# A quarter of the state-times-C products of the last two scan blocks on GpSimd, read from a state that the scan writes to SBUF

## The chip, the cores and the metric

One core of one Trainium2 chip. The metric is the device time of the core in microseconds; the lower the better. Engines are named as in the profile: PE (matrix products), DVE (VectorE), ACT (ScalarE), POOL (GpSimd), SP (the engine that issues most DMAs here).

## The reference

Four layers in a row work on x of 4 sequences x 1024 tokens x 256 channels in float32, each adding its normalised output to x: a linear-attention encoder of four layers, a LoRA mixture, a Mamba layer (a selective state space), and a mixture of 8 experts. The change is in the Mamba layer:

```python
def step(h, inp):
    u, d, b, c = inp
    dA = jnp.exp(d[..., None] * A)
    h = h * dA + (d * u)[..., None] * b[:, None, :]
    y = jnp.einsum('bds,bs->bd', h, c)
    return (h, y)
h0 = jnp.zeros((Bb, D_IN, D_STATE), dtype=x.dtype)
_, ys = jax.lax.scan(step, h0, (u_t, d_t, B_t, C_t))
```

There are D_IN = 512 channels with D_STATE = 16 states each, so the state h has 8192 numbers, and a recurrence along the 1024 tokens of every sequence. After the scan, y goes through a projection and a layer norm; then comes the gating of the experts, and tokens are sent to their expert's slots in memory (disp), worked on, and added into the output by a scatter.

## The kernel before, in words

The kernel builds a list of operations, and a planner (`Program.order`) decides the order on every engine. It goes through the list by a clock of its own: every operation has a cost from a table (`VECTOR_NS`, `GPSIMD_NS`, `SCALAR_NS`), an engine takes the operation that can start first, and buffers of a pool are handed out by their planned times. `emit` then writes all engines' instructions in that order. So each engine runs a fixed queue in order, and one changed cost or one operation on another engine can change the order of everything recorded with it. Where the planner sees PE idle for long it adds idle matrix products (`fill`, seen in the profile as mm<-cst).

Tokens are cut into 8 blocks of 512 (NBLK = 8, TB = 512), two to a sequence (NB = 2; half = 0 for the first). The encoder runs over units of one layer and one block; beside it `stream` feeds the later layers, block after block: `front(j)` makes the inputs of the scan, `scan(j)` does the recurrence, `back(j)` the projection and norms, `route(j)` the gating, and `expert(k)` one expert. The encoder is through before the last blocks; with the scans of blocks 6 and 7 the experts run (from j == NBLK - 2 on). The front of block 7 runs beside the scan of block 6.

`scan(j)` goes over the block's 8192 states in 64 tiles of 128 partitions x 512 tokens; a tile holds 16 channels with 8 states each. The loops are db (4 groups of 128 channels), r (2), q (4) and k (2 halves of the states); k = 0 and 1 make a pair. Each tile takes these steps:

- SP loads dd: delta, and delta times u, spread over partitions (three buffers each, once a pair).
- POOL makes dbu = (delta u) x B (tag dbu, three buffers in SBUF).
- ACT makes h = exp(A delta) in PSUM (`ps_h`, two buffers).
- DVE scans along the tokens: h = h x state + dbu, in place in PSUM (`tensor_tensor_scan`).
- In the first half of a sequence (blocks 0, 2, 4, 6) DVE copies the last column of the state to last_h, from which the second half starts.
- DVE makes hc = h x C (eight buffers in SBUF).
- PE sums hc over the states into y (`sums`, four tiles q side by side).

After the last r, DVE makes ys from y, and POOL multiplies ys by the gate zl. In the profile, bc is the tile of B or C.

Nearly every instruction is recorded by one helper line (L207), so groups are told apart by their tiles. Before the change the steps in question are lines 1259 (dbu), 1266 (scan), 1271 and 1272 (hc).

Of the kernel before, what the change touches and what calls it, by code (L numbers as in the profile page):

```python
# [12 lines left out]
ALU = mybir.AluOpType  # L13
# [8 lines left out]
TB = 512  # L22
NT = TB // P
NBLK = BATCH * SEQ // TB
LAYERS = 4
NB = SEQ // TB
# [408 lines left out]
def sandwich_kernel(ctx: ExitStack, tc: tile.TileContext, io: dict):  # L435
    nc = tc.nc
# [38 lines left out]
    nc = Program(tc)  # L475
# [121 lines left out]
    def layers(ctx: ExitStack):  # L597
# [615 lines left out]
        def scan(j):  # L1213

            half = j % NB
            BC = []
            for side in range(2):
                t = fpool.tile([P, NSH, TB], F32, tag=f"bc{side}", name=f"bc{side}")
                nc.sync.dma_start(
                    t, bcd[j][side].unsqueeze(0).to_broadcast([GC, SH, NSH, TB])  # L1220
                )
                BC.append(t)
            Bt, Ct = BC
            begun.append(j)
            ys = Y[j] = fpool.tile([P, NDB, TB], F32, tag="ys", name="ys")
            for db in range(NDB):
                y = ps_y.tile([P, TB], F32, tag="y", name="y")

                def sums(tiles, r, k):
                    start = r == 0 and k == 0  # L1230
                    stop = r == GQ - 1 and k == NSH - 1
                    nc.side_by_side(
                        [
                            (y[q * 32 : (q + 1) * 32, :], m["gsum"][:, r, :], tiles[q, k], start, stop)
                            for q in range(4)
                        ]
                    )

                late = []
                for r in range(GQ):  # L1240
                    if r == GQ // 2:
                        xl = fpool.tile([P, TB], F32, tag="xl", name="xl")
                        nc.sync.dma_start(xl, xcd[j][db])
                        zl = fpool.tile([P, TB], F32, tag="zl", name="zl")
                        nc.sync.dma_start(zl, zsd[j][db])
                    tiles = {}
                    for q in range(4):
                        g = q * GQ + r
                        gg = db * (P // GC) + g
                        dd = []  # L1250
                        for k in range(2):
                            t = spool.tile([P, TB], F32, tag=f"dd{k}", name=f"dd{k}", bufs=3)
                            nc.sync.dma_start(
                                t,
                                dud[j][db][g * GC : (g + 1) * GC, k, :].unsqueeze(1).to_broadcast([GC, SH, TB]),
                            )
                            dd.append(t)
                        for k in range(NSH):
                            dbu = spool.tile([P, TB], F32, tag="dbu", name="dbu", bufs=3)
                            nc.gpsimd.tensor_tensor(dbu, dd[1], Bt[:, k, :], ALU.mult)  # L1260
                            h = ps_h.tile([P, TB], F32, tag="h", name="h")
                            nc.scalar.activation(
                                h, dd[0], AF.Exp, scale=m["A"][:, gg, k : k + 1]
                            )
                            last = m["last_h"][:, gg, k : k + 1]
                            nc.vector.tensor_tensor_scan(
                                h, h, dbu, 0.0 if half == 0 else last, ALU.mult, ALU.add
                            )
                            if half < NB - 1:
                                nc.vector.tensor_copy(last, h[:, TB - 1 : TB])  # L1270
                            hc = tiles[q, k] = spool.tile([P, TB], F32, tag="hc", name="hc", bufs=8)
                            nc.vector.tensor_tensor(hc, h, Ct[:, k, :], ALU.mult)
                            if late:
                                sums(*late.pop(0))
                        yield 4
                    late = [(tiles, r, k) for k in range(NSH)]
                for args in late:
                    sums(*args)
                t = ys[:, db, :]
                nc.vector.scalar_tensor_tensor(  # L1280
                    t, xl, m["mcol"][:, db, M_D : M_D + 1], y, ALU.mult, ALU.add
                )
                nc.gpsimd.tensor_tensor(t, t, zl, ALU.mult)
                yield 0.8
# [340 lines left out]
        def stream():  # L1625
# [10 lines left out]
            for j in range(NBLK):  # L1636
# [16 lines left out]
                for n, cost in enumerate(scan(j)):  # L1653
                    yield cost
                    post()
                    if extra:
                        if (got := next(extra[0], "end")) == "end":
                            extra.pop(0)
                        else:
                            yield got  # L1660
                    if n % 2 == 0 or j == NBLK - 1:
                        if side:
                            got = next(side[0], "end")
                            if got == "end":
                                side.pop(0)
                            else:
                                yield got
                        elif ready == j and nxt is None and j + 1 in closed:
                            nxt = front(j + 1)
                            side.append(nxt)  # L1670
                            ready = j + 1
# [199 lines left out]
```

## Time and profile before

| what | us |
|---|---|
| median of 3 runs | 2727.3 |
| lowest and highest run | 2727.06, 2740.75 |
| the profiled execution | 2735.95 |
| its span | 2734.1 |
| scan of block 6 on DVE, first start to last end | 2374.3 to 2534.4 |
| scan of block 7 on DVE | 2540.5 to 2705.7 |
| busy in the span: PE, DVE, ACT, POOL | 2524.7, 1726.9, 1590.6, 1325.1 |

The page of the profile gives each engine's busy time and its costliest groups. Over the whole span PE is busy 92% of the time, because the encoder runs for most of it. The last two scan blocks are a stage of their own, from 2374 us to 2706 us, followed by 28 us in which the last block is projected, normalised and stored. What the change is worth is read from this stage alone: the table by stretches gives the busy time of each engine there, the groups say what ended the idle time ahead of each kind of instruction, and the timeline shows the loop.

### The profile page before, as it was taken

How to read it: one execution, taken by the hardware profiler on the slowest of the kernel's cores; microseconds unless marked ns; L12 is line 12 of the kernel's file. 1: busy time of each engine (PE TensorE's matmuls, PEld its weight loads, DVE VectorE, ACT ScalarE, POOL GpSimd, SP SyncE). 2: the span in 40 equal slices, each digit the busy share in tenths (PEclk: the TensorE clock that was granted, in tenths of full speed). 3: DMA queues.
4: the chain of work that ended last, by engine and by line, in shares of the span. 5: the costliest groups of instructions: out<-in, count | busy, mean ns of one | idle time of the engine just before them, and what ended most of it. 6: DMA issues, size and time to landing. Idle time of an engine off the chain costs nothing. (4 is left out here: it accounts for less than half of the span.)

```text
span 2734.1 us, 31975 instructions
## 1 busy us (share of the span) xinstructions
PE 2524.7 (92%) x9794; PEld 1568.9 (57%) x9794; DVE 1726.9 (63%) x3291; ACT 1590.6 (58%) x3309; POOL 1325.1 (48%) x1845
## 2 busy tenths in 40 slices
PE   9999999999999999999999998988998998888996
PEld 6566556656656555556655555555554566444664
DVE  2121322223468766885349887997897994599885
ACT  4434454456676666665666776765765643666443
POOL 1101111123255455564427467764864883467865
PEclk9999999999999999999999999998998999899998
DMA  4011201121354343442245445545444453767762
GB/s 108 27 46 56 66 27 32 51 66 66 105 168 148 104 153 121 147 147 85 85 136 167 134 148 174 177 150 176 135 151 155 129 151 101 246 193 234 207 179 53
DMA packets 202227, 342.18 MB, mean 125 GB/s; under 512 B 32197, under 2 KB 79514, under 8 KB 198976
## 3 DMA queue, kind: packets, MB, share of 16 engines
q1 hardware_dynamic: 197760, 334.80, 39.2%
q0 software_dynamic: 4288, 5.27, 1.1%
q8 instruction: 79, 1.29, 0.2%
q14 instruction: 100, 0.82, 0.1%
HBM read 281.13 MB, written 59.92 MB: 125 GB/s over the span
## 5 line engine op out<-in xcount | busy, mean ns | idle before, releaser
L207 POOL TENSOR_TENSOR dbu<-dd,bc 128x512 f32<-128x512 f32 x512 | 664.2, 1328 | 267.6 <-DVE h L207 224.0
L207 ACT ACTIVATE h<-dd,A 128x512 f32<-128x512 f32 x512 | 344.5, 687 | 295.8 <-DVE hc L207 293.9
L207 PE MATMUL mm<-w,fT 128*128 128x256 f32 x2176 | 490.7, 383 | 5.7 <-ACT t L207 2.7
L207 PEld LDWEIGHTS mm<-w,fT 128*128 128x128 f32 x2176 | 413.8, 192 | 85.8 <-issue 15.5
L207 DVE TENSOR_TENSOR_SCAN h<-h,last_h,dbu 128x512 f32<-128x512 f32 x256 | 321.3, 1279 | 53.1 <-ACT h L207 39.7
L207 DVE TENSOR_TENSOR hc<-h,bc 128x512 f32<-128x512 f32 x512 | 340.8, 679 | 16.3 <-PE y L242 14.7
L207 DVE TENSOR_TENSOR_SCAN h<-h,dbu 128x512 f32<-128x512 f32 x256 | 304.3, 1218 | 33.0 <-ACT h L207 27.1
L398 PE MATMUL mm<-cst 128*128 128x256 f32 x1166 | 274.7, 394 | 7.5 <-DVE qe L207 3.3
L207 PE MATMUL mm<-hT,w1b 128*128 128x512 f32 (+1 forms) x576 | 255.7, 589 | 18.0 <-ACT fT L207 9.1
L207 PE MATMUL mm<-hT,w1a 128*128 128x512 f32 (+1 forms) x576 | 258.3, 596 | 14.5 <-ACT hT L207 12.1
L398 PEld LDWEIGHTS mm<-cst 128*128 128x128 f32 x1166 | 228.3, 198 | 58.3 <-issue 17.2
L207 PE MATMUL mm<-wkv,hT 128*128 128x512 f32 x512 | 228.1, 597 | 8.3 <-DVE qT L207 6.1
L207 ACT ACTIVATE fT<-mm,cols 128x512 f32<-128x512 f32 x256 | 170.8, 681 | 72.1 <-PE mm L207 71.6
L207 DVE TENSOR_TENSOR X<-X,mm 128x512 f32<-128x512 f32 x128 | 87.1, 681 | 185.7 <-PE mm L207 185.4
L207 PEld LDWEIGHTS mm<-hT,w1b 128*128 128x128 f32 x576 | 107.7, 193 | 163.0 <-issue 100.2
L207 POOL TENSOR_TENSOR X<-X,ro 128x1024 f32<-128x1024 f32 x64 | 151.4, 2372 | 80.5 <-ACT tok L207 57.4
L207 POOL TENSOR_SCALAR ve<-mv 128x4 f32<-128x4 f32 (+1 forms) x105 | 20.4, 195 | 345.9 <-DVE mv L207 333.4
L207 PEld LDWEIGHTS mm<-hT,w1a 128*128 128x128 f32 x576 | 108.0, 196 | 137.7 <-issue 93.4
L207 ACT ACTIVATE tok<-X,nb,rs 128x256 f32<-128x256 f32 x288 | 149.6, 591 | 32.7 <-POOL nb L207 31.7
L207 PEld LDWEIGHTS mm<-wkv,hT 128*128 128x128 f32 x512 | 97.2, 191 | 123.4 <-issue 105.4
L207 ACT ACTIVATE tok<-tok,nb,rs 128x256 f32<-128x256 f32 x252 | 131.9, 590 | 48.2 <-POOL nb L207 43.6
L207 ACT ACTIVATE r<-mv,eps 128x4 f32<-128x4 f32 (+1 forms) x105 | 30.9, 295 | 220.5 <-DVE mv L207 220.3
(195 smaller groups left out, 4037.0 us busy)
## 6 DMA issues: line engine op xcount, KB each, us to landing
dd<-dud SPq DMA_DIRECT2D x512, 256.0 KB
w<-in_w_dram SPq DMA_DIRECT2D x16, 1024.0 KB
dud<-t SPq DMA_DIRECT2D x32, 512.0 KB
tok<-in_x_dram SPq DMA_DIRECT2D x16, 512.0 KB
wkv<-in_wkv_dram SPq DMA_DIRECT2D x16, 512.0 KB
w1a<-in_w_dram SPq DMA_DIRECT2D x16, 512.0 KB
w1b<-in_w_dram SPq DMA_DIRECT2D x16, 512.0 KB
t<-in_w_in_dram SPq DMA_DIRECT2D x16, 512.0 KB
```

The lines of the kernel that those rows point to most:

```text
L207: getattr(getattr(self.nc, engine), name)(*map(put, args), **{k: put(v) for k, v in kwargs.items()})
L398: self.nc.tensor.matmul(tile[:, 0:IDLE_COLS], work[:, 0:P], work, start=True, stop=True)
```

## The change

For j >= 6 and q == 3 the scan writes its state to the dbu tile in SBUF, in place of dbu, instead of to h in PSUM. For these tiles the product hc is made on GpSimd, which reads the state and C from SBUF. The copy to last_h reads the state from where it now lies: in block 6 that makes 16 copies out of SBUF. All other tiles stay as they were. Of 64 tiles of a block 16 are concerned, in two blocks 32.

```diff
@@ -1263,13 +1263,17 @@
                                 h, dd[0], AF.Exp, scale=m["A"][:, gg, k : k + 1]
                             )
                             last = m["last_h"][:, gg, k : k + 1]
+
+                            share = j >= NBLK - NB and q == 3
+                            state = dbu if share else h
                             nc.vector.tensor_tensor_scan(
-                                h, h, dbu, 0.0 if half == 0 else last, ALU.mult, ALU.add
+                                state, h, dbu, 0.0 if half == 0 else last, ALU.mult, ALU.add
                             )
                             if half < NB - 1:
-                                nc.vector.tensor_copy(last, h[:, TB - 1 : TB])
+                                nc.vector.tensor_copy(last, state[:, TB - 1 : TB])
                             hc = tiles[q, k] = spool.tile([P, TB], F32, tag="hc", name="hc", bufs=8)
-                            nc.vector.tensor_tensor(hc, h, Ct[:, k, :], ALU.mult)
+                            engine = nc.gpsimd if share else nc.vector
+                            engine.tensor_tensor(hc, state, Ct[:, k, :], ALU.mult)
                             if late:
                                 sums(*late.pop(0))
```

## The prediction

> **What bounds the kernel now.** I read the table of stages first, cut where a state-scan block begins and ends on VectorE (DVE), because the change touches only the last two blocks. Its columns are the stretch, its length, then busy time of PE, PEld, DVE, ACT and POOL, the clock, the DMA share and GB/s:
>
> ```profile
> 2374.20:2534.40 160.20, 141.13 (x546) 75.69 (x544) 153.82 (x249) 105.97 (x227) 114.66 (x107) 0.96 0.77 227
> 2534.40:2540.50 6.10, 6.10 (x34) 4.04 (x31) 1.54 (x5) 1.73 (x5) 2.70 (x4) 1.00 1.05 283
> 2540.50:2705.70 165.20, 154.53 (x690) 104.25 (x688) 139.06 (x208) 77.78 (x177) 118.54 (x127) 0.96 0.55 157
> 2705.70:2734.10 28.40, 8.55 (x42) 5.15 (x36) 11.29 (x27) 6.04 (x16) 10.98 (x31) 0.74 0.13 29
> ```
>
> Block 6 is DVE-bound: 153.82 of 160.20 us, 96%. Block 7 has DVE at 84%, so waits matter there. The last 28 us are a chain of small steps that the change does not touch. PE looks fuller than either, but the groups of PE show 55.1 us of idle fillers (mm<-cst), so it is not the limit. GpSimd (POOL) is at 72% in both blocks.
>
> Next, the groups of DVE in block 7 say what ends its idle time:
>
> ```profile
> L207 DVE TENSOR_TENSOR_SCAN h<-h,last_h,dbu 128x512 f32<-128x512 f32 x64 | 80.3, 1280 | 12.5 <-POOL dbu L207 6.9 <-ACT h L207 5.0 <-issue 0.4
> L207 DVE TENSOR_TENSOR hc<-h,bc 128x512 f32<-128x512 f32 x63 | 41.1, 678 | 5.9 <-PE y L242 5.6
> L207 DVE SCALAR_TENSOR_TENSOR pp<-ex,pp 128x3 f32<-128x3 f32 x4 | 0.7, 176 | 9.5 <-ACT X L207 9.5
> ```
>
> Already 6.9 us go to waiting for GpSimd's dbu, and 15 us to two stalls behind expert work (PE y, ACT X). The groups of GpSimd for blocks 6 and 7:
>
> ```profile
> L207 POOL TENSOR_TENSOR dbu<-dd,bc 128x512 f32<-128x512 f32 x62 | 84.3, 1427 | 25.5 <-DVE h L207 23.1 <-DMA dd<-dud 2.3
> L207 POOL TENSOR_TENSOR dbu<-dd,bc 128x512 f32<-128x512 f32 x63 | 84.9, 1457 | 17.0 <-DVE h L207 4.9 <-DVE short L207 2.9 <-DVE sm_s L207 1.9
> ```
>
> So GpSimd has about 23 us of real slack in block 6 (waiting for the scan to free a dbu buffer) and about 17 us in block 7. Last, the timeline of DVE, where the loop runs undisturbed in block 7, and the rows of tile run, which hold a copy between SBUF tiles:
>
> ```profile
> 2677.70 2.45 DVE L207 TENSOR_TENSOR_SCAN h<-h,last_h,dbu 128x512 f32<-128x512 f32 x2
> 2680.07 1.26 DVE L207 TENSOR_TENSOR hc<-h,bc 128x512 f32<-128x512 f32 x2
> 2681.57 2.47 DVE L207 TENSOR_TENSOR_SCAN h<-h,last_h,dbu 128x512 f32<-128x512 f32 x2 [0.23 <-issue]
> ```
> ```profile
> L207 DVE COPY run<-run x7: 160/164/1872, 1151.8 to 2612.0; 128x8 f32<-128x8 f32 x7
> ```
>
> A pair of tiles costs 3.87 us: two scans (2.38 from start to start of what follows), two products (1.19, so 0.595 each) and 0.23-0.3 waiting for ACT to refill the two PSUM tiles h.
>
> **The change part by part.**
>
> *Removed from DVE.* Per block 4 x 2 x 2 = 16 products hc, 32 in all, at 0.595 us in sequence: 9.5 us a block, 19.0 us together. In block 6 DVE is the limit, so this is on the path.
>
> *Added to GpSimd.* The same 32 products from SBUF. The nearest row is dbu, the same shape and operands: 1.27 us alone, 1.24 us in a row. 16 x 1.25 = 20 us a block: 114.66 becomes 134.7 in block 6, 118.54 becomes 138.5 in block 7. The cover is the 23 and 17 us of slack; 20 us just fits the one and not the other.
>
> *The scan writes dbu in SBUF instead of h.* No row has a scan that writes SBUF. The product reads PSUM and writes SBUF at 678 ns, while mm<-sg,mm writes PSUM at 686 ns: the destination costs nothing there. I take 0 and bound it at +-0.05 us a scan, +-1.6 us in all.
>
> *The h tile comes free after the scan instead of after the product.* ACT's exp for the next pair then no longer waits for hc; the 0.23 us after a shared pair goes, 8 times, in block 7 only (in block 6 other DVE work fills it): -1.8 us. What is late next is dbu: the third row below.
>
> *dbu is held longer.* There are three buffers, and the product on GpSimd now frees two of them. Walk a shared pair in block 7 from its first scan at 0. The scans end at 1.28 and 2.47. GpSimd does hc 1.35-2.6, hc 2.6-3.85, and only then dbu for the second tile of the next pair, 3.85-5.1 (the changed program's GpSimd order has just this: hc, hc, dbu). DVE scans the first tile of the next pair 2.38-3.6, does its product to 4.25, then waits to 5.15, scans, multiplies: 6.95 us at the next pair. Before, the two pairs took 2 x 3.87 = 7.74. The gain is 0.8 us, not 1.19 + 0.23 = 1.42, times 8: 6.4 us in block 7 instead of 9.5 + 1.8. In block 6 about 5.7 us of other DVE work per group of four pairs can fill part of the wait; I take 2 us lost there, so -7.5.
>
> *Port contention grows.* DVE operations with two SBUF inputs, and SBUF-to-SBUF ones with one, stretch when GpSimd is in the middle of an instruction: pp<-qT runs from 147 to 3352 ns, sg<-t from 413 to 2918, run<-run as shown. Those that read PSUM (hc, 652 to 693) do not. Against the short durations of the same groups this stretching costs about 16 us in block 6 and 10 in block 7. GpSimd's busy time grows by about a fifth: +3.3 and +2.1 us. The exposed operations are still the same few dozen small ones.
>
> *The 16 copies of last_h in block 6 now read SBUF.* [...] The nearest row is run<-run, the same operation between SBUF tiles: 0.16 us, and 1.87 us the one time GpSimd was in a long instruction. By this row each copy after a shared scan, just when GpSimd starts its product, may wait for the rest of that product: 0 to 1.25 us, 0 to 20 us in all. The first copy of a pair stands behind the second scan and meets the tail of the first product (0.15 us), the second meets the start or middle of the next one; I put 0.7 us on a pair, 8 x 0.7 = +5.6. [...] No run here shows a one-element copy of SBUF. I take the row, since it is the same operation, and keep 0 and 20 for the range.
>
> *The end of the block.* The last pair's products now end on GpSimd: 1.25 us after the second scan instead of 1.2: +0.2 us. The order also changes around it: in the last groups a scatter (1.5 to 1.7 us on GpSimd) stands just before the last two products and another between them and ys. ys waits for DVE and PE anyway, so 0.
>
> *Moved only.* The order list is planned anew, so expert scatters, PE fillers and some dd loads on SP's queue change places within blocks 6 and 7; the count of SP's instructions is the same. This can move the 9.5 and 5.6 us stalls either way. I take 0 and +-8 us.
>
> **Sum.** Block 6: -7.5 + 3.3 + 5.6 = +1.4. Block 7: -6.4 + 2.1 + 0.2 = -4.1. [...] The profiled execution took 2735.95 us (span 2734.1 and 1.85 around it), which is 8.6 us above the median of the runs, 2727.3; the loops are the same in both, so I set the difference on the median: 2727.3 - 2.7 = 2724.6, say 2725. A measurement of this kernel can tell about 0.5%, 13.6 us, from no change (the runs shown spread by 13.7 us).
>
> **The rivals.**
>
> *Slower: the products block GpSimd's queue.* GpSimd takes its queue in order. A product that stands ahead of dbu waits for its scan, and with it every dbu, scatter and norm step behind it. The price: where the next dbu comes later than DVE could scan it by more than the 1.19 us that the pair saved, the pair is a loss. The walk gives 0.9 us with nothing between. With one scatter (1.6 us) or one product with sg in between it is 2.5 us, and the orders show such neighbours at about half of the 16 pairs. If all 16 lose 2 us of wait: 32 - 19 + 5 contention + 6 copies = +24, about 2750. Block 7 speaks for it: 138.5 us busy plus the 30 us of its idle time that are not buffer slack is 168 us, more than the block's 165. Against it: 23 us slack in block 6. [...]
>
> *Faster: all of it counts.* Copies free, contention unchanged, dbu delays filled with other DVE work: -19.0 - 1.8 = -21, 2706. For: DVE at 96% in block 6. Against: DVE is short of dbu already in block 7.
>
> *Nothing: something else sets the end.* In block 7 the stalls behind expert work absorb what DVE gains (15 us of waits that are PE's and ACT's), and block 6 comes out even: 2727.
>
> **How the numbers follow.** The mixed case 0.45, nothing 0.08, slower by queue or copies 0.28, faster 0.16, the rest split among tails of the mixed case (0.02 slower, 0.01 faster). Faster by over 0.5%: 0.17; within: 0.53; slower: 0.30. The likeliest case is 2725. The range reaches to the full gain below, 2707, and to the queue case above, 2750.
>
> **What would show it.** Right: DVE busy near 147-150 us in block 6 and 131 in block 7, hc on GpSimd at 1.25-1.45 us, last_h copies of SBUF between 0.15 and 1.3 us, more idle of scan on POOL dbu (about 7 us more in block 7). [...]

## The result, and the profile after

| kernel | median, us | runs |
|---|---|---|
| before, beside the runs of after | 2731.6 | 7 |
| after | 2752.1 (2748.7 to 2758.5) | 7 |

The ratio is 1.0074 [1.0059, 1.0088]: the change makes the kernel 20 us slower. The profiled execution of after took 2755.62 us, its span 2753.9.

The table by stretches of after, cut as before at the first and last scan of blocks 6 and 7 (stretch, length, then busy time of PE, PEld, DVE, ACT and POOL with instructions, the clock, the DMA share, GB/s):

```profile
2368.10:2542.20 174.10, 148.58 (x539) 78.13 (x538) 157.75 (x234) 105.12 (x228) 133.08 (x121) 0.89 0.69 206
2542.20:2550.40 8.20, 7.84 (x42) 4.57 (x41) 2.15 (x4) 2.69 (x9) 5.63 (x6) 1.00 1.02 255
2550.40:2725.50 175.10, 156.54 (x690) 105.42 (x688) 135.37 (x193) 77.15 (x173) 138.49 (x143) 0.95 0.52 150
2725.50:2753.90 28.40, 7.64 (x36) 4.91 (x28) 10.16 (x25) 6.03 (x16) 10.64 (x31) 0.70 0.09 23
```

Block 6 grew from 160.2 to 174.1 us, the gap behind it from 6.1 to 8.2, block 7 from 165.2 to 175.1; the last 28.4 us did not change. Between these two profiles the blocks grew by 26 us and the medians by 20: the execution of after came to block 6 some 6 us earlier (2368.1 against 2374.3), though up to there every engine has the same instructions in the same order in both kernels. So much is spread between executions. The surprise stands in the DVE column: block 6 lost 16 products from DVE, and DVE is busy for 157.75 us there, not less than the 153.82 of before. The groups of DVE in block 6 say why. The columns are line, engine, operation, tiles and shapes, count, then busy us and mean ns, then idle us ahead and what ended it. After:

```profile
L207 DVE TENSOR_TENSOR_SCAN h<-h,dbu 128x512 f32<-128x512 f32 x48 | 57.2, 1219 | 7.2 <-ACT h L207 3.7 <-POOL dbu L207 3.5
L207 DVE TENSOR_TENSOR_SCAN dbu<-h,dbu 128x512 f32<-128x512 f32 x16 | 18.7, 1207 | 1.3 <-ACT h L207 0.8 <-issue 0.5
L207 DVE SCALAR_TENSOR_TENSOR xc<-xi,mcol,xc 128x512 f32<-128x512 f32 x12 | 15.8, 1319 | 0.1
L207 DVE TENSOR_SCALAR sg<-t 128x512 f32<-128x512 f32 x4 | 9.4, 2358 | 0.0
```

and two of these groups before:

```profile
L207 DVE SCALAR_TENSOR_TENSOR xc<-xi,mcol,xc 128x512 f32<-128x512 f32 x12 | 11.3, 941 | 0.1
L207 DVE TENSOR_SCALAR sg<-t 128x512 f32<-128x512 f32 x4 | 4.7, 1164 | 1.0 <-ACT t L207 1.0
```

The scan into SBUF takes 1207 ns against 1219 into PSUM, so the scan itself does not pay for the new place of the state. But xc and sg, work of block 7's front that the change does not touch, went from 941 to 1319 ns and from 1164 to 2358. They read and write SBUF while GpSimd is at work. To add this up I take for every DVE operation of block 6 and its gap its duration less the 10th percentile of its own kind (same operation, tiles and shape; scans, products hc, last_h copies and statistics left out), and call the sum *stretching*: 16.5 us before, 29.2 after. DVE's waits over 0.15 us grew beside it from 8.1 to 17.3 us.

In the list of waits (who waited for whom: us, times, longest us) GpSimd had this in block 6 before:

```profile
POOL dbu L207 <- DVE h L207: 23.1, 15, 2.4
```

and after:

```profile
POOL dbu L207 <- DVE h L207: 12.0, 7, 3.5
POOL hc L207 <- DVE dbu L207: 9.4, 6, 4.4
```

The 23.1 us were the "slack" that was to take up 20 us of products. It shrank by only 11 us, and the products brought 9.4 us of waiting of their own: each stands in GpSimd's queue until its scan is done, and everything behind it stands too: the longest of these waits, 4.37 us, ends at 2453.13, and the dbu behind that pair of products starts at 2455.59. In block 7 the groups of DVE after show the waits directly:

```profile
L207 DVE TENSOR_TENSOR_SCAN h<-h,last_h,dbu 128x512 f32<-128x512 f32 x48 | 60.5, 1281 | 19.5 <-POOL dbu L207 18.2 <-ACT h L207 1.3
L207 DVE TENSOR_TENSOR hc<-h,bc 128x512 f32<-128x512 f32 x48 | 31.6, 679 | 13.5 <-PE y L242 8.8 <-DMA bc<-bcd 4.2
```

6.9 us of waiting for dbu became 18.2, and 5.6 us of waiting for PE's sums became 8.8 before hc (5.7 more before ys). On the other side the 9.5 us stall behind ACT's X, which the prediction shows, is down to 0.3; all waits of DVE in block 7 over 0.15 us went from 28.0 to 43.3 us. Two rows by tile show what the new operations cost themselves, the copies of last_h from SBUF and the products on GpSimd (ns, shortest, median, longest):

```profile
L207 DVE COPY last_h<-dbu x16: 122/142/154, 2385.0 to 2542.2; 128x1 f32<-128x1 f32 x16
```
```profile
L207 POOL TENSOR_TENSOR hc<-dbu,bc x32: 1260/1272/1857, 2383.3 to 2725.6; 128x512 f32<-128x512 f32 x32
```

### The profile page after: what moved, and what is told of

It is laid out like the page before. It is cut to its first block, busy times and chain, and to the rows that moved or that the text cites. A ratio compares the mean times of both kernels' runs of the same rounds, so it can differ in the third digit from the quotient of the medians.

```text
span 2753.9 us, 31986 instructions
## 1 busy us (share of the span) xinstructions
PE 2530.1 (92%) x9790; PEld 1570.2 (57%) x9790; DVE 1727.8 (63%) x3259; ACT 1588.7 (58%) x3309; POOL 1364.2 (50%) x1877
## 3 DMA queue, kind: packets, MB, share of 16 engines
q1 hardware_dynamic: 197760, 334.80, 38.9%
## 4 chain that ended last, share of the span: by engine, by line
PE 43%; ACT 19%; DVE 18%; POOL 9%; issue 7%; DMA 3%; SPq 0%; POOLq 0%; DVEq 0%; ACTq 0%
PE mm L207 39%; ACT tok L207 9%; DVE h L207 6%; POOL dbu L207 4%; DVE hc L207 3%; ACT h L207 2%; DVE st L207 2%; PE mm L398 2%; POOL tok L207 2%; POOL t L207 2%; ACT t L207 1%; DVE xc L207 1%; ACT hT L207 1%; ACT fT L207 1%; DVE kv L207 1%
## 5 line engine op out<-in xcount | busy, mean ns | idle before, releaser
L207 DVE TENSOR_TENSOR_SCAN h<-h,last_h,dbu 128x512 f32<-128x512 f32 x240 | 301.2, 1278 | 59.6 <-ACT h L207 35.6
L207 DVE TENSOR_TENSOR hc<-h,bc 128x512 f32<-128x512 f32 x480 | 319.6, 678 | 26.6 <-PE y L242 20.1
L207 DVE TENSOR_TENSOR_SCAN h<-h,dbu 128x512 f32<-128x512 f32 x240 | 285.8, 1218 | 40.0 <-ACT h L207 31.0
L207 PE MATMUL mm<-hT,w1a 128*128 128x512 f32 (+1 forms) x576 | 261.8, 602 | 21.1 <-ACT hT L207 12.5
L207 PE MATMUL mm<-hT,w1b 128*128 128x512 f32 (+1 forms) x576 | 259.1, 596 | 19.2 <-ACT fT L207 9.7
```

The source lines that it names most:

```text
L207: getattr(getattr(self.nc, engine), name)(*map(put, args), **{k: put(v) for k, v in kwargs.items()})
```

## The experiments

The theory from these profiles: *load*. 20 us a block more on GpSimd, which takes its queue in order, lengthen block 6 through every DVE operation and every tile that meets it. Its rivals: the new *order*; the *holding* of dbu; the *port* alone, a name for the stretching of DVE (no trace shows a port; what is measured is how long DVE's operations take); the *scatters*, of which one can wait until the one before has landed (in block 6 of before once, for 2.4 us; they land 3.4 to 7.5 us after their issue there). PE's clock, which falls in block 6 of after, is a further one; no run held it, and the last section says what the traces show of it. The columns of the summary are: ratio to the kernel before, block 6 with its gap, block 7, and for block 6 with its gap GpSimd's busy time, DVE's stretching and DVE's waits over 0.15 us, in us, from one profile each.

| run | ratio [95%] | block 6 | block 7 | POOL | stretch | waits |
|---|---|---|---|---|---|---|
| before | 1 | 166.2 | 165.2 | 117.3 | 16.5 | 8.1 |
| after | 1.0074 [1.0059, 1.0088] | 182.3 | 175.0 | 138.7 | 29.2 | 17.3 |
| e1 | 1.0057 [1.0038, 1.0076] | 180.6 | 161.9 | 138.3 | 27.0 | 20.1 |
| e2 | 1.0119 [1.0095, 1.0144] | 191.8 | 177.1 | 138.6 | 19.9 | 22.5 |
| e3 | 1.0009 [0.9998, 1.0019] | 171.0 | 167.2 | 117.5 | 19.2 | 9.9 |
| e4 | 0.9999 [0.9988, 1.0010] | 169.3 | 163.6 | 117.3 | 17.9 | 9.8 |
| e5 | 1.0069 [1.0046, 1.0092] | 184.7 | 165.8 | 139.2 | 29.7 | 19.2 |
| e6 | 1.0022 [1.0011, 1.0033] | 172.2 | 167.4 | 120.7 | 16.9 | 10.4 |
| e7 | 0.9971 [0.9957, 0.9986] | 162.5 | 164.4 | 114.6 | 4.7 | 18.1 |
| e8 | 1.0045 [1.0032, 1.0058] | 175.3 | 166.1 | 135.2 | 9.6 | 33.2 |
| e9 | 0.9987 [0.9977, 0.9996] | 170.9 | 164.4 | 117.2 | 17.7 | 11.2 |
| e10 | 1.0057 [1.0039, 1.0076] | 178.3 | 167.4 | 139.4 | 26.8 | 16.2 |
| e11 | 1.0037 [1.0018, 1.0056] | 174.8 | 166.1 | 127.6 | 25.7 | 13.4 |
| e12 | 0.9988 [0.9978, 0.9999] | 165.3 | 167.6 | 114.6 | 5.2 | 20.4 |
| e13 | 1.0019 [1.0008, 1.0029] | 164.9 | 167.9 | 133.3 | 10.0 | 22.2 |
| e14 | 1.0084 [1.0065, 1.0103] | 165.9 | 167.6 | 116.8 | 17.0 | 7.0 |
| e15 | 1.0169 [1.0150, 1.0189] | 191.0 | 166.2 | 139.2 | 38.9 | 17.5 |
| e16 | 1.0017 [1.0008, 1.0025] | 167.8 | 165.1 | 107.8 | 13.3 | 5.8 |
| e17 | 1.0060 [1.0044, 1.0076] | 180.9 | 169.3 | 130.3 | 26.6 | 15.3 |

Block 6 with the same operations as before shows 166.2, 169.3, 170.9 and 171.0 us in four profiles (before, e4, e9, e3): differences of less than 5 us between single profiles are not read. Where two runs with their own control are compared, the ratio is the quotient of the two, with the intervals added as independent ones.

**e1, e2: is it the holding of dbu, or the load?** e1 writes the state into the hc tile, and GpSimd multiplies in place, so the product no longer holds a dbu buffer:

```diff
-                            state = dbu if share else h
+                            hc = tiles[q, k] = spool.tile([P, TB], F32, tag="hc", name="hc", bufs=8)
+                            state = hc if share else h
...
-                            hc = tiles[q, k] = spool.tile([P, TB], F32, tag="hc", name="hc", bufs=8)
```

> As the change, but the shared scans write the state to the hc tile and GpSimd multiplies it there in place, so a dbu tile is free again as soon as its scan is done, as before the change. Queue theory (dbu tiles held through the product, next dbu behind two products): DVE's waits for dbu in blocks 6 and 7 fall from 22 us to about 7, the time from 20 us above before to about 5 above. Port theory (DVE operations on SBUF alone wait for GpSimd's instructions): GpSimd does the same work, so the stretching stays at 44 us (27 before) and the time stays 13 to 20 us above before. Re-planning theory: anywhere within 10 us of the change, with waits in other places.

e2 is the kernel before, with dbu of the same 32 tiles made twice on GpSimd:

```diff
-                            nc.gpsimd.tensor_tensor(dbu, dd[1], Bt[:, k, :], ALU.mult)
+                            for _ in range(2 if j >= NBLK - NB and q == 3 else 1):
+                                nc.gpsimd.tensor_tensor(dbu, dd[1], Bt[:, k, :], ALU.mult)
```

> The kernel before, with each dbu of the 32 tiles in question made twice on GpSimd: the load that the change adds there (32 products, 40 us), with no product taken from DVE, no scan to SBUF and nothing on GpSimd that waits for a scan. Port theory: the stretching of DVE rises as in the change, by about 17 us, and the time is 15 to 25 us above before. Queue theory: nothing waits for a scan, GpSimd has 23 and 17 us of slack, so at most 5 to 8 us above before, from dbu that comes late.

Blocks 6 and 7 of e1 in the table by stretches:

```profile
2364.60:2537.20 172.60, 144.35 (x538) 79.84 (x538) 155.68 (x234) 105.23 (x228) 131.71 (x120) 0.88 0.70 208
2545.20:2707.10 161.90, 152.48 (x691) 103.71 (x689) 132.53 (x193) 78.39 (x177) 138.07 (x143) 0.99 0.57 162
```

and of e2:

```profile
2366.60:2545.00 178.40, 153.22 (x541) 82.74 (x541) 157.76 (x248) 104.69 (x228) 134.04 (x122) 0.86 0.66 200
2558.40:2735.50 177.10, 165.10 (x711) 111.93 (x710) 148.84 (x208) 76.70 (x173) 140.21 (x145) 0.95 0.48 139
```

With dbu not held, block 7 is back (161.9 us) with GpSimd just as busy, but block 6 keeps its length and the loss is still 1.0057. (e3 below holds dbu in block 7 and has 167.2 us there, so the 175.0 of after are not the holding alone.) Load without the change costs more than the change itself: +0.0119, 32 us [26, 39], more than either theory gave it. The rest of the change thus gives some 12 us back, net of what it costs besides the load. The loads are not quite alike: e2's extra operation stands ahead of its own scan, the product of the change behind it.

Nor does e2's load show where one would look for it. Three waits of its block 6:

```profile
POOL dbu L207 <- DVE h L207: 27.8, 15, 3.4
DVE h L207 <- ACT h L207: 12.3, 11, 2.3
DVE h L207 <- POOL dbu L207: 1.7, 1, 1.7
```

GpSimd still waits 27.8 us for DVE to free a buffer, more than the 23.1 before; DVE hardly waits for dbu, but 12.3 us for ACT's h (1.6 before), and its stretching rose by 3.4 us only. ACT, whose queue holds h and the experts' steps, waited 26.3 us for PE ahead of fT (15.9 before).

**e3, e5, e4: in which block, and is it the order?** e3 shares only in block 7 (`share = j == NBLK - 1 and q == 3`), e5 only in block 6 (`j == NBLK - 2`). e4 leaves the kernel before as it is but tells the planner that these 32 products take 60 ns more, so that it writes another order:

```diff
-                            nc.vector.tensor_tensor(hc, h, Ct[:, k, :], ALU.mult)
+                            op = nc.vector.tensor_tensor(hc, h, Ct[:, k, :], ALU.mult)
+                            if j >= NBLK - NB and q == 3:
+                                op.busy, op.done = op.busy + 60, op.done + 60
```

> The change in block 7 alone; block 6 is as before but for the planner's order at its end. Queue theory: block 7 was 10 us longer with 12 us more waiting for dbu, so 8 to 12 us above before. Port theory: block 7 has few operations that read SBUF alone (stretching 10.7 before, 14.9 with the change), so 4 us of stretching against 9.5 us of products saved, 0 to 5 us below before.

> The kernel before; only the planner's cost of the 32 products in question is 60 ns higher, which orders the last two blocks anew without other work. Re-planning theory: the time moves by 5 to 20 us either way. Queue and port theory: within 5 us of before.

> The changed kernel with only block 6 shared (16 products on GpSimd instead of 32). Theory (the loss comes from the added GpSimd load in block 6, where DVE has no idle time to lose): the loss stays nearly whole, +15 to +20 us against the kernel before; block 6 with the gap behind it is near 180 us (166.2 before, 182.3 with both blocks shared) and block 7 near 165. Rival (the two blocks act on each other, the loss needs both): +10 us or less, since block 7 shared alone was +2.5 us.

Block 7 of e3, then block 6 of e5:

```profile
2545.50:2712.70 167.20, 154.36 (x696) 104.47 (x694) 135.72 (x193) 78.18 (x177) 138.49 (x143) 0.98 0.57 157
```
```profile
2369.20:2546.00 176.80, 150.17 (x539) 78.95 (x538) 158.50 (x233) 105.44 (x227) 133.53 (x121) 0.88 0.67 202
```

The same 20 us of load are a loss of 0.0009, not told from none, in block 7 and of 0.0069, 19 us, in block 6: the whole of it. My reading is that in block 7 DVE, with 84% of the time to do and 28 us of waits, can hide something, and in block 6 with 96% it cannot. That block 7 of after took 10 us longer in its profile is thus no cost of block 7's products alone. The new order of e4 costs nothing, but it is a mild one: between the first scans of blocks 6 and 7, ACT's queue, which the change does not touch, differs from before in 18 places in e4 and in 36 in after. The order of after with the old work was not tried.

**e6: the scan into SBUF alone.** The state goes to dbu, but the product stays on DVE, which then reads two SBUF inputs; GpSimd's load is as before.

```diff
-                            nc.vector.tensor_tensor(hc, h, Ct[:, k, :], ALU.mult)
+                            engine = nc.vector
+                            engine.tensor_tensor(hc, state, Ct[:, k, :], ALU.mult)
```

> The scan of the 32 tiles writes its state into the dbu tile in SBUF, as in the change, but the product stays on DVE, which now reads two SBUF inputs. GpSimd's load is as before. Theory of the port (a DVE operation with two SBUF inputs waits for the end of the GpSimd instruction that is running): GpSimd is busy 72% of these blocks and half of a dbu of 1.27 us is 0.64, so 0.46 us a product, 7.4 us a block and 10 to 15 us in all; hc<-dbu on DVE shows 0.68 to 1.9 us. Rival (only GpSimd's load counts, exposure is cheap but behind a scatter): 0 to +4 us. Either way the scan into SBUF itself stays at 1.21 to 1.28 us.

The row by tile of these products:

```profile
L207 DVE TENSOR_TENSOR hc<-dbu,bc x32: 658/678/4416, 2385.8 to 2710.1; 128x512 f32<-128x512 f32 x32
```

Half of the 32 took no more than 678 ns, the time of a product from PSUM; 30 took under 700, one 2845 and one 4416 ns. Together they lost 6.2 us, and the time is 0.0022, 6 us, longer: under the estimate of the port theory (10 to 15), over its rival's. Exposure alone is not the 20 us.

**e7, e8: the port.** In the front of block 7 the convolution is summed in PSUM and sg<-t is made on ACT, so that these 16 DVE operations leave GpSimd's way. e7 is this in the kernel before, e8 in the one after.

```diff
...
-                t = xc[:, db, :]
+                off = j == NBLK - 1
+                t = ps if off else xc[:, db, :]
...
-                nc.vector.tensor_scalar(v1, e, 1.0, -1.0, ALU.add, ALU.add)
+                if j == NBLK - 1:
+                    nc.scalar.activation(v1, e, AF.Identity, bias=1.0)
+                    nc.scalar.activation(v1, v1, AF.Identity, bias=minus)
+                else:
+                    nc.vector.tensor_scalar(v1, e, 1.0, -1.0, ALU.add, ALU.add)
...
```

> The kernel before, but in the front of block 7 (which runs in the scan of block 6) the convolution is summed in PSUM instead of SBUF (12 steps xc<-xi,mcol,xc then have one SBUF input) and the 4 steps sg<-t are made on ACT in two steps each. It is the control for the next run. Both theories: DVE loses 4.7 us of sg<-t and 2.5 us of stretching of xc in block 6, so -4 to -7 us against before; if ACT or PE is what sets the pace there, 0.

> The same edit of the front in the changed kernel. Theory of the port: sg<-t and xc<-xi,mcol,xc took 9.3 us of the 12.7 us that stretching grew in block 6, so with them out of GpSimd's way the loss against the control run falls from 20 us to 8 to 12 us. Rival (the loss is waiting in GpSimd's in-order queue and what follows from it on ACT and PE): the loss against the control stays at 17 to 21 us.

The groups of DVE in block 6 of e7:

```profile
L207 DVE TENSOR_TENSOR_SCAN h<-h,dbu 128x512 f32<-128x512 f32 x64 | 75.8, 1219 | 6.2 <-ACT h L207 4.8 <-POOL dbu L207 1.4
L207 DVE SCALAR_TENSOR_TENSOR mm<-xi,mcol,mm 128x512 f32<-128x512 f32 x12 | 9.0, 747 | 0.0
```

and of e8:

```profile
L207 DVE TENSOR_TENSOR_SCAN h<-h,dbu 128x512 f32<-128x512 f32 x48 | 57.6, 1221 | 16.0 <-POOL dbu L207 9.5 <-ACT h L207 6.5
L207 DVE TENSOR_TENSOR_SCAN dbu<-h,dbu 128x512 f32<-128x512 f32 x16 | 19.1, 1212 | 3.1 <-POOL dbu L207 2.7
L207 DVE SCALAR_TENSOR_TENSOR mm<-xi,mcol,mm 128x512 f32<-128x512 f32 x12 | 9.0, 749 | 0.1
```

The edit works: the convolution takes 747 and 749 ns with and without the change. Yet the loss against the control is 1.0045 / 0.9971 = 1.0074 [1.0055, 1.0094], as large as before. Most of the stretching is gone (9.6 us instead of 29.2) and waiting for dbu has come in its place: 12.2 us (9.5 and 2.7) against 1.4. The port theory as I put it has failed. How I read it: while an operation of DVE is stretched, GpSimd gets its dbu done; without the stretching DVE arrives earlier and waits for the dbu. Stretching and waiting would then be two forms of one shortage.

**e9, e10: the scatters.** The experts' scatters write to four scratch arrays in turn, with the order of all instructions kept; e9 is this in the kernel before, e10 in the one after.

```diff
...
+            to = dst
+            if op == ALU.add:
+                to = aside[len(turns) % 4]
+                turns.append(0)
             nc.nc.gpsimd.indirect_dma_start(
-                out=dst,
+                out=to,
```

> The kernel before, with the same order of instructions on every engine, but the experts' scatters go to four scratch arrays in turn instead of out, so that none has to wait until the one before it has landed. What it leaves out is the adding of the experts' outputs into out. It is the control for the next run. Theory of the scatter chain: in block 6 of before GpSimd waits 3.5 us ahead of such scatters, mostly hidden: 0 to -4 us against before. Theories of port and of load: 0.

> The same edit in the changed kernel (it also leaves out the adding of the experts' outputs into out). Theory of the scatter chain (a scatter waits at the head of GpSimd's queue until the scatter before it has landed, 3 to 10 us after its issue, and with more work on GpSimd DVE has no dbu in reserve to bridge that): the loss against the control falls from 20 us to under 10 us. Rival (the load and the port alone): the loss stays at 16 to 21 us.

1.0057 / 0.9987 = 1.0070 [1.0049, 1.0091]: the loss stays, so it is not the waiting of one scatter for another.

**e11: half of it.** Only k = 1 of each pair is shared (`... and q == 3 and k == 1`).

> The changed kernel with only the second tile of each pair shared (k = 1): 16 products on GpSimd in two blocks instead of 32. If the loss goes with the load: half of it, +8 to +12 us. If it comes with two products in a row ahead of the next dbu (two of three dbu buffers held): 0 or a gain, -5 to +4 us.

Block 6 of e11:

```profile
2368.50:2534.90 166.40, 142.56 (x538) 78.21 (x536) 158.79 (x241) 105.02 (x227) 121.46 (x113) 0.93 0.69 213
```

Half of the products, half of the loss: 0.0037 [0.0018, 0.0056], 10 us. It goes with the load and does not need two products in a row.

**e12: a version to beat both.** The edit of e7, and sharing in block 7 alone with the state in hc.

> A version to beat both kernels: the front of block 7 off GpSimd's way as in the control run e7, and in block 7 alone a quarter of the products on GpSimd, from a state that the scan leaves in the hc tile. If the two gains add up (e7: -7 us; state in hc: block 7 shorter by 3 us): -9 us against before, 2723 to 2725. If block 7 is limited by waits for dbu and PE: as e7, 2727 to 2729.

The gains do not add up: 0.9988 is no better than e7's 0.9971 (the intervals overlap). The best version of the study is e7, 0.29% [0.14, 0.43] faster than the kernel before, and that is the control's edit, without the change.

**e13: no stretching and no holding.** The edits of e8 and e1 together.

> The edit of e8 (front of block 7 off GpSimd's way) and that of e1 (state of the shared tiles in the hc tile, so that dbu is not held by the product) together, in both blocks; the control is e7 (2727.5, 0.9971). If stretching and the holding of dbu are the whole loss: 0 to +5 us against e7, 2727 to 2733. If the bare load of 20 us a block on a queue taken in order costs time in whatever form: +12 to +17 us against e7, 2739 to 2745, with DVE still waiting near 10 us for dbu in block 6.

Against its control e7 the loss is 1.0019 / 0.9971 = 1.0048 [1.0030, 1.0066], 13 us. Against e8 it is 0.0026 less [0.0009, 0.0043]: the holding of dbu was worth some 7 us once the stretching was out of the way. In block 6 DVE's waits for dbu fell from 12.2 to 2.2 us; this half of the expectation for the load ("still waiting near 10 us for dbu") was wrong, though the loss it named was right. Other waits are longer: for ACT's h 9.8 us in block 6 (4.8 in e7), for dbu 12.5 and for PE's y 13.5 us in block 7 (2.0 and 5.7 in e7; but e7 has the 9.5 us behind ACT's X there, and e13 0.3). These profiles do not show where the 13 us lie. Block 6 is only 2.4 us longer than in e7, block 7 3.5 and the end behind it 1.7; another 6.0 us between the two executions lie ahead of block 6. So without stretching and holding the load hardly lengthened block 6 in the one profile taken, while the medians still tell a loss.

**e14, e15: more dbu in reserve.** Four dbu buffers and seven of hc (`bufs=3` to 4, `bufs=8` to 7); e14 before, e15 after.

> The kernel before with four dbu buffers instead of three and seven hc buffers instead of eight (there is no more room in SBUF). Control for the next run. Expected by all: 0 to -4 us if the 6.9 us of waiting for dbu in block 7 shrink; +3 us if seven hc buffers make DVE wait for PE.

> The same buffers in the changed kernel. If the loss is a lack of dbu in reserve (DVE waits whenever GpSimd is late by more than one tile): the loss against the control falls to under 12 us, and block 6 comes near 172 us. If load and port set it: it stays at 16 to 21 us.

The two buffer counts together cost 0.0084, which nobody expected, so these are poor kernels. The counts hold for all blocks, and in e14 the time is lost ahead of block 6, which starts at 2387.8 us; what a fourth dbu buffer alone does stays open. But 1.0169 / 1.0084 = 1.0084 [1.0057, 1.0112] says that with four the change loses 23 us, no less than with three, and e15 has the most stretching of all, 38.9 us.

**e16, e17: take other work off GpSimd.** The eight steps sg<-t,sg and sg<-sg,t of block 7's front go to DVE; e16 before, e17 after.

```diff
-                nc.gpsimd.tensor_tensor(v1, e, v1, ALU.subtract)
-                nc.gpsimd.tensor_tensor(v1, v1, lv, ALU.add)
+                engine = nc.vector if j == NBLK - 1 else nc.gpsimd
+                engine.tensor_tensor(v1, e, v1, ALU.subtract)
+                engine.tensor_tensor(v1, v1, lv, ALU.add)
```

> The kernel before, but the eight steps sg<-t,sg and sg<-sg,t of the front of block 7 (11.8 us of GpSimd in block 6) run on DVE. Control for the next run. DVE is 96% busy in block 6, so 8 x 0.68 = 5.4 us more, less what GpSimd no longer stretches: +1 to +6 us by every theory.

> The same edit in the changed kernel: GpSimd then has 126 to 128 us of work in block 6 with the gap behind it, instead of 138.7, as in the run with one product of a pair. If the loss goes with GpSimd's load in block 6, whatever the work is: it falls to +7 to +13 us against the control. If it belongs to the shared products themselves (each waits for its scan at the head of the queue, and two stand ahead of the next dbu): it stays at 16 to 21 us.

Block 6 of e16, then of e17:

```profile
2369.50:2531.10 161.60, 140.35 (x533) 76.02 (x532) 155.34 (x257) 105.45 (x227) 104.96 (x98) 0.95 0.77 223
```
```profile
2366.50:2539.80 173.30, 151.43 (x536) 79.76 (x536) 159.10 (x240) 105.06 (x227) 125.81 (x113) 0.88 0.70 206
```

The products are all there, and the loss is 1.0060 / 1.0017 = 1.0043 [1.0025, 1.0061], 12 us. It falls when other work leaves GpSimd, as the load theory said (7 to 13), though the interval, 7 to 17 us, touches the rival's lower end (16). From e16 to e17 GpSimd's busy time with the gap rose from 107.8 to 130.3 us; the price of load seems less where GpSimd starts from less.

## Why the prediction was wrong

The forecast was 2725 us, and the median is 2752.1, just above the upper end of the range, 2750.

*The step that failed: "Added to GpSimd ... The cover is the 23 and 17 us of slack".* It priced 20 us a block of GpSimd work as covered, with 5.4 us of contention and some 7 us of late dbu as the remainder, 12.5 us in all. e2 measured such a load by itself, though ahead of the scans: 32 us. The slack was no stock to be drawn on: it was 15 waits of at most 2.4 us in block 6, it shrank by 11 of the 23.1 us in after, and in e2 it even grew, to 27.8, while block 6 with its gap became 26 us longer. That GpSimd was late where the experts' and the front's steps come between, so that a product put there pushes all of its queue, is a reading of this and was not tested. In block 7 the slack was misread besides: of the 17.0 us that GpSimd sat idle ahead of dbu, the row that the prediction shows gives 4.9 to a scan freeing a buffer.

What block 6 with its gap shows in place of the forecast +1.4 us is +16.1. DVE's busy time went from 155.3 to 159.9 us: -10.8 for 16 products at 678 ns, +12.7 of stretching, +2.7 in all else. Its idle time went from 10.9 to 22.4.

*Removed from DVE, -19.0.* The products left DVE (48 of 64 remain in the groups). What they were worth in time no run measured by itself; e2 and after, 32 and 20 us, put all of the change but its load at -12 us, with the holding of dbu and the waits behind scans in it.

*Port contention grows, +3.3 and +2.1.* Measured as stretching, it grew by 12.7 us in block 6 and by 4.2 in block 7 (10.7 to 14.9): a load higher by a fifth did not stretch by a fifth. e8 shows besides that this term cannot be added to the others: removed, it comes back as waiting.

*dbu held longer.* Not settled in block 7, where the prediction walked through it. The waits for dbu grew by 11.8 us there, where 7 had been said, and e1, which takes the hold away, has 161.9 us instead of 175.0 and 10.8 us of these waits; but e3, which holds dbu in block 7, has 167.2 us and 10.4. In the loss e1 is 0.0017 below after, within the intervals. From e8 to e13 the hold is worth 7 us, and there the waits that fell are those of block 6.

*PE set aside.* The 55.1 us of fillers, by which PE was said not to be the limit, all stand in block 7: in block 6 PE is busy 141.13 of 160.20 us, 88%, without a filler. PE, its clock and the steps that wait for it were thus put at nothing there without a reason (see the last section).

*The copies of last_h, +5.6.* Wrong: all 16 took 122 to 154 ns, no longer than the copies out of PSUM (126 to 160), also where GpSimd was in the middle of a product (2386.83: 0.14 us, beside hc from 2386.35 to 2388.05). The prediction's sentence on what stretches in the middle of a GpSimd instruction is thus too wide: these SBUF-to-SBUF copies did not. The row run<-run, 128x8, was the nearest in kind and does not carry over to 128x1; why, no run shows. With 0 here the sum would have been -8.3, further from the result: this error hid part of the other.

*Scan into SBUF, 0; end of the block, +0.2; moved only, 0.* Right: 1207 against 1219 ns; the tail is 28.4 us in both; e4, with its mild new order, gave 0.9999. *h comes free earlier, -1.8:* waits for ACT's h in block 7 went from 5.0 to 4.0 us, in block 6 from 1.6 to 4.5, so there is hardly a gain.

*What was to show it.* DVE busy 147 to 150 us in block 6 was forecast and is 157.75; this row alone refutes the sum for block 6. The products at 1.25 to 1.45 us were right.

*The slower rival* had the size, +24, and the engine, but the wrong place: it looked for waits for dbu in block 7 and held the 23 us of block 6 against itself. e3 and e5 show the reverse. Its size came from 16 pairs that lose 2 us each and from 6 us of copies that cost nothing, so that it came near is in part luck.

With the forecast -19.0 for the products, 32 us of load (e2) and 7 of holding (e8 to e13) the sum is +20, as measured. This agreement proves little: the pieces come from different kernels, and the first was not measured. What is shown is that added work on GpSimd in block 6 brings the loss (e2, e3, e5, e11, and e17 less sharply). Not settled: by which chain the load reaches the end, and how much of it goes through the new order or PE's clock. Taking away stretching or scatter waits changed the form of the delay more than its size.

## What to carry to other kernels

Here the idle time of an engine with a queue in order was no stock of capacity (23.1 us in 15 waits of at most 2.4 us, which shrank by 11 when 20 us of products came): look where it lies and how long each wait is, and whether the work added stands there. Before giving such an engine work, double an operation that it already has (as e2 does) and time that: it tells whether more load is free there, though not its exact price at another place of the queue. Count an engine's idle fillers in the stage where the change is, not in the one beside it. When a stretching or a wait is to be counted, ask what comes next in its place: of two terms with one source, both must not be added, nor both taken off.

## What was not expected of the hardware

**A DVE operation can last through several GpSimd instructions.** In block 6 of after five operations lost more than 2 us each, some 19 of the 29.2 us of stretching; before there were two, with 5.7 of 16.5 us. Each lasted through two or more GpSimd instructions in a row. Two of them in the timeline of after (start, us, engine, line, operation), DVE and POOL:

```profile
2407.79 4.36 DVE L207 TENSOR_TENSOR pp<-qT 128x3 f32<-128x3 f32 x1
...
2428.60 0.72 DVE L207 SCALAR_TENSOR_TENSOR xc<-xi,mcol,xc 128x512 f32<-128x512 f32 x1
...
2430.09 5.19 DVE L207 SCALAR_TENSOR_TENSOR xc<-xi,mcol,xc 128x512 f32<-128x512 f32 x1
```
```profile
2405.69 2.77 POOL L207 TENSOR_TENSOR hc<-dbu,bc 128x512 f32<-128x512 f32 x2
2408.15 3.97 POOL L207 TENSOR_TENSOR dbu<-dd,bc 128x512 f32<-128x512 f32 x3
...
2429.49 1.50 POOL L538 DMA_INDIRECT out_dram<-X,own  x1 [0.88 <-DVE last_h L207]
2430.45 4.26 POOL L207 TENSOR_TENSOR dbu<-dd,bc 128x512 f32<-128x512 f32 x3
```

The step xc takes 0.72 us, and then 5.19 us, from a scatter over three dbu to 0.57 us past the end of the last. The small step pp (147 ns at its shortest) takes 4.36 us, from a product over three dbu. In both rows DVE's operation ends just behind the end of a GpSimd instruction, by 0.57 and 0.03 us, and the one of xc outlasts four of them. Why it ends behind that one and not behind one of those before was not tried.

**PE at half its clock while it is 80% busy.** Three stretches of after, and PE's timeline in the last of them:

```profile
2418.00:2424.00 6.00, 2.21 (x7) 1.01 (x7) 5.83 (x10) 3.89 (x8) 5.84 (x6) 0.90 0.96 283
2424.00:2430.00 6.00, 4.91 (x13) 1.78 (x14) 5.91 (x10) 2.53 (x6) 3.81 (x4) 0.53 0.79 216
2442.00:2448.00 6.00, 4.95 (x8) 2.34 (x8) 4.73 (x9) 2.04 (x4) 3.00 (x3) 0.50 0.66 196
```
```profile
2442.53 2.50 PE L207 MATMUL mm<-hT,w1b 128*128 128x320 f32 x4 [0.53 <-ACT fT L207]
2445.55 2.50 PE L207 MATMUL mm<-hT,w1b 128*128 128x320 f32 x4 [0.53 <-ACT fT L207]
```

In the first stretch PE is busy for 2.21 of 6 us, with a wait of 3.04 us that ends at 2420.67; in the next the granted clock is 0.53. From 2430 to 2436 it is 1.00, with PE busy for 2.67 us; then, behind a wait of PE of 3.79 us, it is 0.54 and 0.50 in the next two stretches of 6 us, with PE busy for 5.00 and 4.95. In the last of these PE and ACT pass small steps to each other: four products take 2.50 us, where four of the same take 1.34 in block 6 of before at a clock of 1.00, then ACT's fT follows, and then the next four. A round lasts 3.02 us, and ACT makes one h in each, while DVE in the undisturbed loop takes one every 1.94 us (half a pair). So here the slow clock delays h, and DVE waits for it (1.27 us at 2446.18).

Over block 6 the clock is 0.89, against 0.96 before. It is lower than the control's in every run whose block 6 with its gap is over 7 us longer: e1 0.88, e2 0.86, e5 0.88, e11 0.93 (before 0.96); e10 0.89 (e9 0.95); e15 0.87 (e14 0.97); e17 0.88 (e16 0.95); e8 0.90 (e7 0.91). The last pair says that block 6 can become 13 us longer with almost the same clock, so a further fall of the clock is not needed for a loss. In the others a longer block may bring waits of PE such as the two of over 3 us ahead of the falls above, or a slow PE may lengthen the block; no run here held the clock up to tell the two apart.
